# A recurrent layer with expert routing: another order of the first loads, softmax moved into the scan, more expert work inside the search

## The chip, the cores and the metric

The kernel runs on one core of one Trainium2 chip. The metric is the time of one execution on the device in microseconds (us); lower is better. The time before is the median of 3 runs.

## What is computed

A GRU runs over T = 256 steps with B = 16 sequences and D = 512 features. Its states go through a router with E = 16 experts in which each expert chooses its 256 best tokens of 4096; the experts share one weight matrix. All in float32. Cut to what matters:

```python
def cell(h, x):
    gi = x @ W_ih + b_ih                 # [16, 1536]
    gh = h @ W_hh + b_hh
    r = sigmoid(i_r + h_r); z = sigmoid(i_z + h_z)
    n = tanh(i_n + r * h_n)
    return (1 - z) * n + z * h
hs = scan(cell, cond, x over 256 steps)  # [16, 256, 512]

S = softmax(hs @ router_w + router_b)    # 4096 tokens x 16 experts
G, idx = top_k(S.T, 256)                 # each expert takes 256 tokens
y = scatter_add(idx, G * (hs[idx] @ expert_w + expert_b))
out = x + y
```

Since the expert matrix is shared, the kernel multiplies every token by `expert_w` once and scales the result by the sum of the weights that chose the token (its gate).

## The kernel before

**Tiles.** The 256 steps form NG = 32 groups of TG = 8 steps; a group is 128 rows (16 sequences x 8 steps). `xs` holds x and later the output by group, `ht` the transposed states by group, `lg` the router's logits and later the softmax, `wih` and `whh` the two weight matrices of the GRU, `ewr` the router's and the experts' weights. The input of the scan comes a second time, in another layout: `xa`, loaded by pairs of steps (4 pairs in a group), turned on VectorE into `xT` (`turn_x`, L255). `xa` has one buffer, so the load of the next group's `xa` waits for the turn of the last.

**Order.** The order within the engines is written out by hand (`manual_schedule`), for the head on SyncE, ScalarE and GpSimd (L264), then TensorE and VectorE (L459), in the scan and behind it on all of them.

**Head.** SyncE and ScalarE issue the weights (`load_rows`, L230). GpSimd issues pair 0 of x (`load_pair`, 4 loads, L268), three bias loads (L284), the condition's four (L287) and pair 1 of x (4 loads); SyncE issues pairs 2 and 3 behind the weights, then group 1 (`load_xa`, L238). GpSimd and SyncE can each have only a fixed number of loads under way before the next waits for one to land, as the profile shows. TensorE zeroes the PSUM banks of the gates with `begin_sums` (L112), is kept busy with more of it (`keep_clock`), multiplies pair 0 by the input weights (`x_part`, L429: 32 wide products `ra` for two gates, 32 narrow ones `zz`), makes the biases (`biases`, L310), and multiplies pair 1. VectorE turns pair 0, copies the biases (L472 to L474), turns pair 1 and then the condition (L479, L480), which is the first state.

**Scan.** In step s TensorE multiplies the state by the three gates' weights (`h_part`, L442), then does work for later: `x_part` of the next pair, logits of finished groups (L342) and a quarter of an expert product (`expert`, L391). ScalarE takes the sigmoid r (L504), two tanh (L555) and the sigmoid z (L556), and in even steps puts the biases into the next pair's banks (L406 to L417). VectorE does the products and turns (L508 to L576) that end in the next state. At the end of step c = 3 of a group it turns the next group's x (L595).

**Expert products.** 15 early groups are multiplied inside the scan. The other 17, the late groups, are multiplied behind it, in parts of 256 columns and one eighth of a group: `late_part` (L139, four products, one for each quarter of the PSUM rows). A late group needs a PSUM tile that `late_begin` zeroes (if fresh) and presets with the expert bias (L159, ScalarE); there are five tiles in turn, two of the pool `ps_m` and three of `ps_e`. `expert_for(n)` emits n parts at that point of TensorE's order. A finished group is copied by ScalarE to `ht` (L176), or, once the gate is known, read by VectorE from PSUM.

**Behind the scan.** The last logits (L356), 4 parts, exponential and sum of the 28 old groups (`exp_sum`, L621, L622), the last 4 groups' logits less their maximum (`less_max`, L368 to L374), the old groups' reciprocal and product (`softmax`, L614, L616), then the same for the 4 new groups. TensorE transposes the result (L728, L729).

The search finds each expert's 256th largest weight bit by bit, in 17 rounds (bits 27 to 11, `by_bits`): VectorE counts the weights not below a candidate (L655), TensorE adds the counts over an expert's rows (L670), VectorE drops or keeps the bit (L673, L678). In each round TensorE has 2 or 3 expert parts beneath:

```python
top = by_bits(KNOWN, HIGH, LOW, counts, lambda bit: expert_for(2 + bit % 2))
```

Then the exact threshold is made from the largest of the rest (L738 to L756), and the gate (L698, L702). From there `store` writes group after group: VectorE adds gate times product to x (L708) and SyncE issues the write (L711), early groups first, then the late ones as their parts end. Ahead of the last three groups the count is checked once more: VectorE counts, TensorE sums (L775), VectorE compares, TensorE sums again (L779); a flag chooses whether a slow exact path runs (it does not here).

Of the kernel before, what the change touches and what calls it, by code (L numbers as in the profile page):

```python
# [18 lines left out]
def kernel(  # L19
# [112 lines left out]

    def late_part(g, pe, part):

        k, h = divmod(part, 2)
        cols = slice(HD * h, HD * (h + 1))
        for j in range(KC):
            q = slice(QD * j, QD * (j + 1))
            nc.tensor.matmul(  # L139
                pe[q, cols],  # L140
                ht[:, g, k, q],
                ewr[:, k, E:][:, cols],
                start=False,
                stop=(k == KC - 1),
                tile_position=(0, QD * j),
                skip_group_check=True,
            )

    late = []
    late_sums = {}  # L150
    late_done = []
    gated = []

    def late_begin(pool, fresh=True):
        g = late_groups[len(late_done) + len(late)]
        pe = pool.tile([P, D], F32, name="pe", tag="pe")
        if fresh:
            begin_sums(pe)
        nc.scalar.copy(pe, eb)  # L159
        late.append((g, pe))  # L160

    def late_parts():
        for i, g in enumerate(late_groups):
            _, pe = late[0]
            for part in range(2 * KC):
                late_part(g, pe, part)
                if part == KC and i + 2 < len(late_groups):
                    n = (i + 2) % 5
                    late_begin(ps_m if n < 2 else late_pool[0], fresh=i < 3)
                if part == 2 * KC - 1:  # L170
                    late.pop(0)
                    late_done.append(g)
                    if gated:
                        late_sums[g] = pe
                    else:
                        nc.scalar.copy(wide(g), pe)  # L176
                yield

# [8 lines left out]
    with (  # L187
# [25 lines left out]

        ra = [ps_g.tile([P, 2, P], F32, name=f"ra{i}") for i in range(2)]
        hn = [ps_g.tile([P, 2 * P], F32, name=f"hn{i}") for i in range(2)]
        zz = [ps_g.tile([P, P], F32, name=f"zz{i}") for i in range(2)]

# [46 lines left out]
        with tc.manual_schedule(engines={ET.SP, ET.Activation, ET.Pool}):  # L264
            def load_pair(p, qs):

                for j in range(KC):
                    qs[j % 2].dma_start(  # L268
                        out=xa0[quadrant(j), p, :],
                        in_=x[:, 2 * p : 2 * p + 2, j * P : (j + 1) * P].rearrange("b o d -> o b d"),  # L270
                    )

            for i, gate in enumerate((0, 2, 1)):
                load_rows(wih[:, :, i, :], w_ih[:, gate * D : (gate + 1) * D], "(p c) n -> p c n")
            for gate in (0, 2, 1):
                load_rows(whh[:, :, gate, :], w_hh[:, gate * D : (gate + 1) * D], "(c p) n -> p c n")

            load_pair(0, (nc.gpsimd, nc.gpsimd))
            for dst, src in (
                (b_raw[0:1], b_ih.rearrange("(o g d) -> o g d", o=1, d=D)),  # L280
                (b_raw[1:2], b_hh.rearrange("(o g d) -> o g d", o=1, d=D)),
                (b_n, b_hh[2 * D :].rearrange("(o d) -> o d", o=1)),
            ):
                nc.gpsimd.dma_start(out=dst, in_=src)  # L284
            nc.gpsimd.memset(c0, 0.0)
            for j in range(KC):
                nc.gpsimd.dma_start(  # L287
                    out=c0[QD * j : QD * j + B, :].rearrange("b (c i) -> b c i", c=KC), in_=columns(cond, j)
                )
            load_pair(1, (nc.gpsimd, nc.gpsimd))  # L290
            for p in range(2, TG // 2):
                load_pair(p, (nc.sync, nc.sync))
            for j in range(KC):
                load_xa(1, xa1, j, (nc.sync, nc.sync))
            nc.sync.dma_start(out=ewr[:, :, E:], in_=expert_w.rearrange("(c p) n -> p c n", c=KC))
            nc.sync.dma_start(out=ewr[:, :, 0:E], in_=router_w.rearrange("(c p) n -> p c n", c=KC))
            nc.sync.dma_start(out=rb, in_=router_b.rearrange("(o e) -> o e", o=1).to_broadcast([P, E]))
            nc.sync.dma_start(out=eb, in_=expert_b.rearrange("(o d) -> o d", o=1).to_broadcast([P, D]))
# [67 lines left out]
        def less_max(h, pl):  # L366
# [12 lines left out]
            )  # L379

        pes = {}

# [76 lines left out]
        with tc.manual_schedule(engines={ET.PE, ET.DVE}):  # L459
            for i in range(2):  # L460
                for bank in (ra[i].rearrange("p g d -> p (g d)"), hn[i], zz[i]):
                    begin_sums(bank)
            keep_clock(22)
            turn_x(0, xa0, slice(0, 1))
            for z in (False, True):
                for k in range(KC):
                    x_part(0, k, z)
            keep_clock(2)
            biases(1)
            biases(0)  # L470
            keep_clock(2)
            nc.vector.tensor_copy(bias[:, 0:2, :], ra[1])  # L472
            nc.vector.tensor_copy(nb, hn[1][:, 0:P])
            nc.vector.tensor_copy(bias[:, 2, :], zz[1])  # L474
            turn_x(0, xa0, slice(1, 2))
            for z in (False, True):
                for k in range(KC):
                    x_part(1, k, z)
            nc.vector.transpose(turned, c0)  # L479
# [8 lines left out]
        with tc.manual_schedule(engines={ET.PE, ET.Activation, ET.DVE, ET.Pool, ET.SP}):  # L488
# [4 lines left out]
            for s in range(T):  # L493
# [38 lines left out]
                if s == T - 1:  # L532
                    logits(hn[0][:, P:], range(KC), range(NG - 1, NG), slice(0, TG - 1))


# [71 lines left out]
                if s in (T - 6, T - 4):  # L607
                    late_begin(ps_m)


            old, new = slice(0, NG - KC), slice(NG - KC, NG)

            def softmax(gs):
                nc.vector.reciprocal(tot[:, gs], tot[:, gs])  # L614
                n = gs.stop - gs.start
                nc.vector.tensor_tensor(  # L616
                    lg[:, :, gs], lg[:, :, gs], tot[:, gs].unsqueeze(1).to_broadcast([P, E, n]), ALU.mult
                )

            def exp_sum(gs):  # L620
                nc.scalar.activation(lg[:, :, gs], lg[:, :, gs], AF.Exp)  # L621
                nc.vector.tensor_reduce(tot[:, gs], lg[:, :, gs].rearrange("p e g -> p g e"), AX.X, ALU.add)  # L622

# [3 lines left out]
            )  # L627
            expert_for(4)
            exp_sum(old)
            less_max(NG // KC - 1, hn[0][:, P:])  # L630
            softmax(old)
            exp_sum(new)
            softmax(new)


    with (
# [69 lines left out]

        def store(g, sums, gate):
            nc.vector.scalar_tensor_tensor(  # L708
                xs[:, g, :], sums, gate[:, g : g + 1], xs[:, g, :], ALU.mult, ALU.add
            )  # L710
            nc.sync.dma_start(out=out[:, g * TG : (g + 1) * TG, :], in_=xs[:, g, :])  # L711

# [10 lines left out]
        with tc.manual_schedule(engines={ET.PE, ET.Activation, ET.DVE}):  # L723
# [8 lines left out]
            nc.vector.tensor_copy(by_block[:, KC - 1], ps_last.rearrange("p (q i) -> p q i", q=QG))  # L732

            counts = ps_c.tile([P, HIGH - LOW + 1], F32, name="counts")
            top = by_bits(KNOWN, HIGH, LOW, counts, lambda bit: expert_for(2 + bit % 2))

# [30 lines left out]
            gated.append(True)  # L767
            for i, g in enumerate([g for g in range(NG) if g not in late_groups] + late_groups):
                while g in late_groups and g not in late_done:
                    expert_for(1)  # L770
                store(g, late_sums.get(g, wide(g)), gate)
                if i == NG - 4:

                    n = ps_n.tile([P, 1], F32, name="n", tag="n")
                    nc.tensor.matmul(n, same_h, count(kth, "cnt"), start=True, stop=True)  # L775
                    wrong = wk.tile([P, 1], F16, name="wrong")
                    nc.vector.tensor_scalar(wrong, n, float(TOPK), None, ALU.not_equal)
                    n_wrong = ps_n.tile([1, 1], F32, name="n_wrong", tag="n")
                    nc.tensor.matmul(n_wrong, wrong, wrong, start=True, stop=True)  # L779
                    nc.vector.tensor_copy(flag, n_wrong)  # L780

        again = nc.values_load(flag, min_val=0, max_val=P)
        with tc.If(again > 0):
# [54 lines left out]
            for g in range(NG):  # L838
                sums = wide(g)
                if g in late_sums:  # L840
                    sums = ps_e.tile([P, D], F32, name="pe", tag="pe")
                    begin_sums(sums)
                    nc.scalar.copy(sums, eb)
                    for part in range(2 * KC):
                        late_part(g, sums, part)
                store(g, sums, gate)
# [31 lines left out]
```

## Time and profile before

| what | value |
|---|---|
| median of 3 runs | 1173.38 us (1172.32 to 1174.1) |
| the profiled execution | 1174.32 us, of which its span is 1172.5 us |
| mean granted TensorE clock | 0.994 |
| TensorE busy | 1150.8 us, 98% of the span |
| VectorE busy | 702.3 us, 60% |
| ScalarE busy | 332.7 us, 28% |
| first product with a state (L442) | 23.37 us from the span's start |
| last state written (L576) | 1090.62 us |
| transposes behind the softmax (L728) | 1094.80 us |
| last expert product ends | 1166.75 us |

The profile is one execution. Times are from the start of the span. A row of the timeline gives start, duration, engine, line, operation, what is written from what, how often, and in brackets how long the engine was idle before and what released it. Rows of one line that follow each other are merged, so the duration of a row with x24 spans all of them. A float32 product of TensorE is two records.

### The profile page before, as it was taken

The numbers are of one execution on the slowest core, as the hardware profiler recorded it, in microseconds if no ns is written. First come the engines' busy times: TensorE is split into PE (matmuls) and PEld (weight loads), VectorE is DVE, ScalarE is ACT, GpSimd is POOL, SyncE is SP. The second block draws the span as 40 slices with busy tenths as digits, with TensorE's granted clock in tenths as the row PEclk, the third lists the DMA queues.
The fourth block names the chain that finished last, engine by engine and source line by source line (L and its number), as shares of the span: only waits on it lengthen the run. The fifth ranks groups of instructions, "written<-read, shape, count | busy, mean of one in ns | idle before, by whom it ended". The sixth has DMA issues, their size and how long they took to land.

```text
span 1172.5 us, 79871 instructions
## 1 busy us (share of the span) xinstructions
PE 1150.8 (98%) x36285; PEld 1018.5 (87%) x36285; DVE 702.3 (60%) x4077; ACT 332.7 (28%) x1438; POOL 99.9 (9%) x412
## 2 busy tenths in 40 slices
PE   8999999999999999999999999999999999999897
PEld 5899999999999999999999999999999999998454
DVE  1665665666566656666666566666665566656682
ACT  0223323322233323232323232323232323233211
POOL 3000010000000000000000000000000000000000
PEclk8999999999999999999999999999999999999999
DMA  7200000000000000000000000000000000000045
GB/s 231 73 23 20 20 18 23 20 21 20 21 20 20 20 21 20 20 21 20 21 20 20 20 21 20 20 20 22 19 21 20 21 21 19 20 14 13 3 127 164
DMA packets 48712, 38.04 MB, mean 32 GB/s; under 512 B 7952, under 2 KB 40528, under 8 KB 48368
## 3 DMA queue, kind: packets, MB, share of 16 engines
q1 hardware_dynamic: 46128, 29.56, 8.7%
q8 instruction: 285, 4.67, 1.6%
q10 hardware_dynamic: 1632, 3.15, 0.8%
q14 instruction: 59, 0.48, 0.1%
q0 software_dynamic: 608, 0.19, 0.1%
HBM read 24.47 MB, written 8.39 MB: 28 GB/s over the span
## 4 chain that ended last, share of the span: by engine, by line
PE 93%; DVE 3%; DMA 2%; issue 1%; ACT 0%; SPq 0%; POOL 0%; DVEq 0%; ACTq 0%; POOLq 0%
PE ra L442 19%; PE hn L442 19%; PE ra L429 19%; PE zz L442 19%; PE zz L429 9%; PE pe L391 4%; PE pe L139 3%; DMA xa<-in_x_dram 1%; DVE xs L708 1%; PE hn L342 1%; DVE ge L655 1%; SPq L238 0%; POOL xa L268 0%; DMA out_dram<-xs 0%; PE counts L670 0%
## 5 line engine op out<-in xcount | busy, mean ns | idle before, releaser
L442 PE MATMUL ra<-whh,hs 128*16 128x128 f32 (+1 forms) x8192 | 318.5, 273 | 2.9 <-DVE zT L565 1.7
L442 PE MATMUL hn<-whh,hs 128*16 128x128 f32 (+1 forms) x8192 | 318.3, 273 | 0.2
L429 PE MATMUL ra<-wih,xt 128*32 128x256 f32 x4096 | 270.4, 381 | 3.6 <-DVE xt L255 3.1
L442 PE MATMUL zz<-whh,hs 128*16 128x128 f32 (+1 forms) x8192 | 271.0, 273 | 0.0
L504 ACT ACTIVATE r<-ra 128x128 f32<-128x128 f32 x256 | 71.1, 278 | 616.3 <-PE ra L442 616.3
L442 PEld LDWEIGHTS ra<-whh,hs 128*16 128x16 f32 (+1 forms) x8192 | 229.9, 103 | 6.8 <-DVE hs L576 3.3
L508 DVE COPY seen<-r 1x1 f32<-1x1 f32 x256 | 36.3, 142 | 330.3 <-ACT r L504 330.3
L442 PEld LDWEIGHTS hn<-whh,hs 128*16 128x16 f32 (+1 forms) x8192 | 230.8, 103 | 2.2 <-DVE l L368 2.2
L442 PEld LDWEIGHTS zz<-whh,hs 128*16 128x16 f32 (+1 forms) x8192 | 227.5, 103 | 0.1
L429 PEld LDWEIGHTS ra<-wih,xt 128*32 128x32 f32 x4096 | 128.5, 111 | 50.2 <-DVE xt L255 4.0
L555 ACT ACTIVATE t<-t 128x64 f32<-128x64 f32 x512 | 102.9, 248 | 131.7 <-DVE t L553 131.7
L429 PEld LDWEIGHTS zz<-wih,xt 128*32 128x32 f32 x4096 | 117.8, 110 | 23.3 <-DMA wih<-in_L_cond_W_ih_dram 1.3
L429 PE MATMUL zz<-wih,xt 128*32 128x128 f32 x4096 | 136.6, 274 | 0.4 <-DMA wih<-in_L_cond_W_ih_dram 0.4
L562 DVE STREAM_TRANSPOSE nT<-t 128x64 f32<-128x64 f32 x512 | 100.3, 234 | 49.5 <-ACT t L555 49.5
L565 DVE STREAM_TRANSPOSE zT<-zs 128x64 f32<-128x64 f32 x512 | 121.4, 237 | 0.2 <-issue 0.2
L576 DVE TENSOR_TENSOR hs<-v,nT 128x32 f32<-128x32 f32 x512 | 101.5, 198 | 21.7
L573 DVE TENSOR_TENSOR v<-u,zT 128x32 f32<-128x32 f32 x512 | 104.3, 204 | 8.9
L391 PE MATMUL pe<-ewr,ht 128*32 128x128 f32 x1920 | 93.8, 273 | 0.0
L551 DVE TENSOR_TENSOR t<-r,hn 128x64 f32<-128x64 f32 x512 | 89.5, 216 | 0.0
L553 DVE TENSOR_TENSOR t<-t,ra 128x64 f32<-128x64 f32 x512 | 87.9, 213 | 0.0
L568 DVE TENSOR_TENSOR u<-hs,nT 128x32 f32<-128x32 f32 x512 | 78.2, 153 | 0.0
L391 PEld LDWEIGHTS pe<-ewr,ht 128*32 128x32 f32 x1920 | 59.5, 110 | 19.4
(112 smaller groups left out, 569.4 us busy)
## 6 DMA issues: line engine op xcount, KB each, us to landing
xs<-in_x_dram SPq DMA_DIRECT2D x128, 64.0 KB
out_dram<-xs SPq DMA_DIRECT2D x32, 256.0 KB
xa<-in_x_dram SPq DMA_DIRECT2D x248, 32.0 KB
wih<-in_L_cond_W_ih_dram SPq DMA_DIRECT2D x3, 512.0 KB
wih<-in_L_cond_W_ih_dram ACTq DMA_DIRECT2D x3, 512.0 KB
whh<-in_L_cond_W_hh_dram SPq DMA_DIRECT2D x3, 512.0 KB
whh<-in_L_cond_W_hh_dram ACTq DMA_DIRECT2D x3, 512.0 KB
ewr<-in_L_ffn_expert_w_dram SPq DMA_DIRECT2D x1, 1024.0 KB
```

The costliest lines, as they stand in the source:

```text
L391: nc.tensor.matmul(pes[g][quadrant(j), at : at + P], ht[:, g, k, quadrant(j)], ewr[:, k, E + P * quarter : E + P * (quarter + 1)], start=( ...
L429: nc.tensor.matmul(dst, lhs, rhs, start=False, stop=(k == KC - 1), tile_position=(0, QD * j), skip_group_check=True)
L442: nc.tensor.matmul(dst[quadrant(j, m)], lhs, columns(whh[:, k, gate_, :], j), start=False, stop=(k == KC - 1), tile_position=(0, QD * j), ...
L504: nc.scalar.activation(r, ra[p % 2][:, 0, :], AF.Sigmoid)
L551: nc.vector.tensor_tensor(t[half], r[:, cols], hn[p % 2][:, cols], ALU.mult)
L553: nc.vector.tensor_tensor(t[half], t[half], ra[p % 2][:, 1, cols], ALU.add)
L555: nc.scalar.activation(t[half], t[half], AF.Tanh)
L562: nc.vector.transpose(nT[half], t[half])
L565: nc.vector.transpose(zT[half], zs[:, halves[half][1]])
L568: nc.vector.tensor_tensor(u[half], hs[:, halves[half][2], slot(s), :], of_step(nT[half], odd), ALU.subtract)
L573: nc.vector.tensor_tensor(v[half], u[half], of_step(zT[half], odd), ALU.mult)
L576: nc.vector.tensor_tensor(hs[:, halves[half][2], slot(s + 1), :], v[half], of_step(nT[half], odd), ALU.add)
```

## The change

Four things are altered.

1. In the head, GpSimd issues the three bias loads first, then pairs 0 and 1 of x interleaved (8 loads), then the condition. SyncE's 8 loads of pairs 2 and 3 are interleaved in the same way. TensorE makes the biases first, then the wide products of both pairs, then the narrow ones, then two rounds of clock keeping. The six gate banks are whole tiles of 512 columns and are zeroed whole.
2. The softmax of the 28 old groups runs in four stages at the end of steps 240 to 243 (exponential; sum; reciprocal; product), with a sigmoid of one element behind the exponential. Behind the scan only the 4 new groups are left.
3. Late parts: one in each of steps 254 and 255, 5 behind the scan, 2 behind the transposes, 3 in every round of the search. PSUM tiles after the first two are not zeroed again. `late_begin` for the group after next is called when a group ends, not in its middle. Once the gate is known a product has 512 columns.
4. The last late group is done in two halves of 256 columns, each with its own store. The check of the count is spread over the fifth, fourth and third groups from the end: its count, its first sum and its second sum stand each behind another group's parts.

```diff
@@ late parts
+    late_items = [(g, whole) for g in late_groups[:-1]] + [(late_groups[-1], half) for half in halves_d]
-    def late_begin(pool, fresh=True):
+    def late_begin(pool, fresh=False):
@@ late_parts()
-        for i, g in enumerate(late_groups):
-            _, pe = late[0]
-            for part in range(2 * KC):
-                late_part(g, pe, part)
-                if part == KC and i + 2 < len(late_groups):
-                    n = (i + 2) % 5
-                    late_begin(ps_m if n < 2 else late_pool[0], fresh=i < 3)
+        for i, (g, cols) in enumerate(late_items):
+            pe = late[0]
+            for k in range(KC):
+                for part in [cols] if gated or cols != whole else halves_d:
+                    late_part(g, pe, k, part)
+                    if k == KC - 1 and part.stop == cols.stop:
+                        if i + 2 < len(late_items):
+                            late_begin(ps_m if (i + 2) % 5 < 2 else late_pool[0])
...
@@ gate banks
-        ra = [ps_g.tile([P, 2, P], F32, name=f"ra{i}") for i in range(2)]
-        hn = [ps_g.tile([P, 2 * P], F32, name=f"hn{i}") for i in range(2)]
-        zz = [ps_g.tile([P, P], F32, name=f"zz{i}") for i in range(2)]
+        banks = [ps_g.tile([P, D], F32, name=f"gates{i}") for i in range(6)]
+        ra = [bank[:, 0 : 2 * P].rearrange("p (g d) -> p g d", d=P) for bank in banks[0:2]]
+        hn = [bank[:, 0 : 2 * P] for bank in banks[2:4]]
+        zz = [bank[:, 0:P] for bank in banks[4:6]]
@@ loads
-            load_pair(0, (nc.gpsimd, nc.gpsimd))
             for dst, src in (  # the three biases
...
                 nc.gpsimd.dma_start(out=dst, in_=src)
+            load_pairs(0, 2, nc.gpsimd)
             nc.gpsimd.memset(c0, 0.0)
...
-            load_pair(1, (nc.gpsimd, nc.gpsimd))
-            for p in range(2, TG // 2):
-                load_pair(p, (nc.sync, nc.sync))
+            load_pairs(2, TG // 2 - 2, nc.sync)
@@ head on TensorE and VectorE
             keep_clock(22)
-            turn_x(0, xa0, slice(0, 1))
-            for z in (False, True):
-                for k in range(KC):
-                    x_part(0, k, z)
-            keep_clock(2)
             biases(1)
             biases(0)
-            keep_clock(2)
...
-            turn_x(0, xa0, slice(1, 2))
+            for pair in range(2):
+                turn_x(0, xa0, slice(pair, pair + 1))
             for z in (False, True):
-                for k in range(KC):
-                    x_part(1, k, z)
+                for pair in range(2):
+                    for k in range(KC):
+                        x_part(pair, k, z)
+            keep_clock(2)
@@ scan
+                if s >= T - 2:
+                    expert_for(1)
...
+                if T - 16 <= s < T - 12:
+                    softmax(slice(0, NG - KC), s - (T - 16))
+                    if s == T - 16:
+                        nc.scalar.activation(seen[0:1, 0:1], seen[0:1, 0:1], AF.Sigmoid)
@@ behind the scan
-            expert_for(4)
-            exp_sum(old)
+            expert_for(5)
             less_max(NG // KC - 1, hn[0][:, P:])
-            softmax(old)
-            exp_sum(new)
-            softmax(new)
+            for stage in range(4):
+                softmax(slice(NG - KC, NG), stage)
@@ search
+            expert_for(2)
             counts = ps_c.tile([P, HIGH - LOW + 1], F32, name="counts")
-            top = by_bits(KNOWN, HIGH, LOW, counts, lambda bit: expert_for(2 + bit % 2))
+            top = by_bits(KNOWN, HIGH, LOW, counts, lambda bit: expert_for(3))
@@ stores
+            items = [(g, whole) for g in early_groups] + late_items
...
+                step = i - (len(items) - 6)
+                if step == 1:
+                    nc.tensor.matmul(n, same_h, cnt, start=True, stop=True)
+                elif step == 2:
+                    nc.tensor.matmul(n_wrong, wrong, wrong, start=True, stop=True)
+                store(g, late_sums.get((g, cols.start), wide(g)), gate, cols)
+                if step == 0:
+                    cnt = count(kth, "cnt")
+                elif step == 1:
+                    nc.vector.tensor_scalar(wrong, n, float(TOPK), None, ALU.not_equal)
+                elif step == 2:
+                    nc.vector.tensor_copy(flag, n_wrong)
```

## The prediction

> **What bounds the kernel now.** I read the page first (the chain that ended last and the row of clock), then the head, one loop step and the tail in the timeline. The chain says whose time it is:
>
> ```profile
> PE 93%; DVE 3%; DMA 2%; issue 1%; ACT 0%; SPq 0%; POOL 0%; DVEq 0%; ACTq 0%; POOLq 0%
> ```
>
> TensorE's own stream sets the time, so an edit gains what it takes out of that stream or out of the holes in it. The holes are in the head and the tail. The head (start, duration, engine, line, what, idle before it):
>
> ```profile
> 8.33 0.54 POOL L287 DMA_DIRECT2D xs<-in_cond_dram  x1 [1.85 <-DMA xa<-in_x_dram]
> 10.68 2.48 POOL L268 DMA_DIRECT2D xa<-in_x_dram  x4
> 18.79 0.40 DVE L255 STREAM_TRANSPOSE xt<-xa 128x128 f32<-128x128 f32 x1 [1.30 <-DMA xa<-in_x_dram]
> 19.25 3.42 PE L429 MATMUL ra<-wih,xt 128*32 128x256 f32 x32 [0.77 <-DVE xt L255]
> 23.37 0.61 PE L442 MATMUL ra<-whh,hs 128*16 128x128 f32 x16
> ```
>
> GpSimd has eight loads under way; the ninth (8.33) waits for the first to land. So pair 1 of x leaves only at 10.68 and is turned at 18.79, and its 32 products take 3.42 us where 1.71 is the full-clock price (24 such take 1.29 in the loop's chain). The state reaches TensorE at 23.37. The loop, at step 240, on ScalarE:
>
> ```profile
> 1027.43 0.28 ACT L556 ACTIVATE zs<-zz 128x128 f32<-128x128 f32 x1
> 1028.11 0.26 ACT L417 COPY zz<-bias 128x128 f32<-128x128 f32 x1
> 1030.27 0.28 ACT L504 ACTIVATE r<-ra 128x128 f32<-128x128 f32 x1 [1.89 <-PE ra L442]
> ```
>
> ScalarE is free from 1028.37 to 1030.27: 1.90 us. The tail:
>
> ```profile
> 1089.22 1.28 ACT L621 ACT_TABLE_LOAD   x1
> 1090.52 0.58 ACT L621 ACTIVATE lg<-lg 128x448 f32<-128x448 f32 x1
> 1091.13 0.96 DVE L622 TENSOR_REDUCE tot<-lg 128x28 f32<-128x448 f32 x1 [0.25 <-ACT lg L621]
> 1092.00 0.31 DVE L368 STREAM_TRANSPOSE l<-hn 128x128 f32<-128x128 f32 x1
> 1094.80 0.60 PE L728 MATMUL ps<-ident,lg 128*128 128x128 f32 x3 [2.12 <-DVE lg L616]
> ...
> 1110.31 0.16 PE L670 MATMUL counts<-cnt,same_h 128*128 128x1 f16 x1 [0.24 <-DVE ge L655]
> 1111.84 0.18 PE L670 MATMUL counts<-cnt,same_h 128*128 128x1 f16 x1
> 1113.25 0.16 PE L670 MATMUL counts<-cnt,same_h 128*128 128x1 f16 x1 [0.24 <-DVE ge L655]
> ...
> 1127.91 15.32 PE L139 MATMUL pe<-ewr,ht 128*32 128x256 f32 x280
> 1142.95 3.22 ACT L159 COPY pe<-eb 128x512 f32<-128x512 f32 x5 [16.59 <-DVE xs L708]
> 1155.77 0.16 PE L775 MATMUL n<-cnt,same_h 128*128 128x1 f16 x1 [1.60 <-DVE ge L655]
> 1156.19 10.56 PE L139 MATMUL pe<-ewr,ht 128*32 128x256 f32 x192
> ```
>
> Look at three things. TensorE idles 2.12 us before the transposes, behind the softmax of 28 old groups. A round of the search takes 1.53 us with three expert parts (1110.31 to 1111.84, TensorE-bound) and 1.41 with two (to 1113.25, where the count waits 0.24 us for VectorE). After the search TensorE is the bound to the end: 1127.91 to 1166.75, with the check of the count in its way (1154.16 to 1156.19).
>
> **Head: -0.65 us.** GpSimd now issues three bias loads, then the eight of pairs 0 and 1, then the condition's four. Eight may be under way, so five of x leave by about 6.1 us and the other three wait for the biases. Bias loads landed 6.6, 6.6 and 7.4 us after issue, so these three leave between 8 and 10, instead of up to 13.2 for the last of x now. That one landed in 5.5 us after its issue; I put x at 15 to 15.6. The condition's loads move behind it: issued by about 13, landed by about 19, with 0.5 us of turning: hidden if products last beyond 20. SyncE's eight loads keep their waits on weights. TensorE then does the biases at about 9, idles some 5 us, and from 15.3 has 64 wide (3.42 us at full clock) and 64 narrow products (1.74). An idle of 2.28 us (8.52 to 10.80) was followed, by the granted clock in windows of 1 us, by half clock from 12 to 15.3, so I let the first 3.6 us run at half clock, to 18.9: 1.8 us of work done, 3.36 left, two clock-keeping rounds 0.42: the state's product at 22.7 against 23.37. Ends: x a microsecond earlier gives -1.2; half clock until 20.4, or x at 16.5, gives 0 to +0.3. The wider zeroing of six banks (+0.7 us) lies before the biases land. A gain here passes on: pairs 2 and 3 leave SyncE by 24.2 and are turned at 32.1 without a wait, and the second group's load waits for that turn, so the later stall (turn at 40.43) moves along.
>
> **Loop: +1.5 us.** At step 240 ScalarE adds, behind its presets, a table load, the exponential, a table load back and a 1x1 sigmoid: 1.28 + 0.58 + 1.28 + about 0.2 (estimate, nearest row: the smallest ACTIVATE, 0.25) = 3.4 from 1028.37, so r of step 241 starts at 1031.77 instead of 1030.27. Behind it wait VectorE's gate chain and the next state. The first half of the state was there at 1032.58 and TensorE took it at 1032.85, so 0.27 is covered and TensorE stalls 1.23. Here a rule speaks against the change. The Trainium skill, ScalarE: Activation LUTs, What ACT_TABLE_LOAD costs, counts 2.66 us for a switch, the 1.28 of the load and a drain of 1.38. The trace has the 1.28 (1089.22), yet zs ends at 1089.21 and the exponential starts at 1090.52: no drain beside it. By the rule the two switches add 2.8 us more, a stall of 4.0; I take the trace's and keep the other as the end of the range. VectorE's share: the sum (0.96) at step 241 and the reciprocal (0.32) at 242 fit the gap between the state (r + 2.93) and the next gate (r + 4.44). At step 243 the turn of x ends at r + 4.30 and the product (0.62) behind it delays the next gate by 0.5, of which 0.27 is covered: +0.25. One part each in steps 254 and 255 fills holes of 0.42 and 0.49 with 0.44: +0.1, told with the tail.
>
> **Tail: -10.4 us + 0.1.** Softmax: the last table load stays hidden (it starts before the state is ready). l can start at 1091.0, when the last logits are done; to the end of lg 1.12 us as now, exponential 0.29, sum to product 0.75, 0.14 to TensorE: transposes at 1093.3 instead of 1094.8, -1.5. The five parts beneath end at 1093.1.
>
> Search: first count 2.02 us after the transposes as now, 1095.3; two new parts (0.88) fit under it. Sixteen periods of 1.535 = 24.56, instead of 25.25 (1096.82 to 1122.07): the eight rounds with a third part cost 0.12 each, +1.0; the zeroing of three banks goes (0.7 with its slow start); and the two first rounds (2.70 and 1.73 at half clock after 3.4 us of holes) become full-clock ones, since those holes are filled. From last count to the run at 1127.91 nothing changes, 5.84. So the run starts at 1125.7, 2.2 earlier.
>
> Rest: 53 of 136 parts are done there now, 83 follow in 36.46 us (15.32 + 10.57 + 10.57): 0.439 each. Changed: 2 + 5 + 2 + 51 + 6 = 66 done, 70 left = 30.75. Matmuls of 512 columns cost what two of 256 do (128 columns took 0.218, 256 took 0.44: no fixed part to save). The check no longer stops TensorE (its inputs come a group earlier): -2.0, its two products remain, 0.2. The wait for a PSUM bank stays: VectorE must write 23 groups (0.667 each) before the first that frees a bank, TensorE has 38 parts for that time: 0.4, as now. TensorE ends at 1125.7 + 30.75 + 0.6 = 1157.1, not 1166.75: -9.7. Behind it, half a group is stored instead of one: VectorE 0.75 to about 0.4, and the transfer 2.69 to about 2.35 (128 KB less at the 0.3 to 0.4 us that they take at 307 to 400 GB/s): -0.7.
>
> **Sum.** -0.65 + 1.5 + 0.1 - 10.4 = -9.45. Against the profiled execution: span 1172.5 and 1.82 around it, 1174.32, so 1164.9. That execution stands 0.94 above the median 1173.38; from the median the sum gives 1164.0, my time.
>
> **The rivals.**
> - As worked out, 0.76: 1164.0, own range 1161 to 1167.
> - The switch has the drain, or three parts in each round cost 1.7 instead of 1.535 (+2.6), 0.10: 1166.7. For it: a round's TensorE work is nearly all of its period. Against: three-part rounds of 1.53 stand in the trace.
> - The writes become the bound, 0.09: 8.39 MB leave from 1126.5 on. At the 307 GB/s that the windows of 10 us show from 1140 to 1150 that is 27.3 us, before TensorE's end; at 271 (1130 to 1140) 31 us and the last store queues behind it: about +2.5, 1166.5.
> - Slower, 0.03: the clock stays at half in the search. A three-part round then takes about 3.0, 1.5 more; from the seventh such round on the gain is gone, and with all 17 it is 1189. For it: rounds 27 and 26 ran so. Against: the same windows have the granted clock at 1.00 from 1110 on with a TensorE less loaded than it will be.
> - The reorder in the head and the steps' parts do less than said, and all the tail's small terms fail, 0.02: 1172, no change.
>
> **How the numbers follow.** 0.2% (2.3 us) is about what a measurement of this kernel can tell from no change. Faster: 0.76 + 0.10 + 0.09 = 0.95; same 0.02; slower 0.03. The range for 8 in 10: the head from -1.2 to +0.3, the loop from +0.8 to +4.3, the tail from -11.3 to -9.0, not all at one end: 1160.8 to 1167.8.
>
> **What would show it.** Right: pair 1 turned at 15 to 16; the state's first product near 22.7; two table loads at step 240 and one TensorE hole of about 1.2 us behind; transposes 2.7 us after the last state instead of 4.2; all counts 1.53 apart; 35 us from the start of the long run of parts to the end of the span (now 44.6), with no count check in front of parts. Wrong: rounds of 1.7 or more, a drain of more than a microsecond beside a table load, a last store that waits for earlier ones, or a clock of 0.5 after 1097.

## The result, and the profile after

| | before | changed |
|---|---|---|
| median | 1173.74 us (1172.32 to 1176.06, 4 runs) | 1164.78 us (1164.32 to 1165.21, 4 runs) |
| ratio | | 0.9922 [0.9904, 0.9939] |
| profiled execution | 1174.32 us, span 1172.5 | 1164.63 us, span 1162.8 |
| mean granted TensorE clock | 0.994 | 0.996 |

The change takes 8.96 us between the medians, where the working summed to 9.45. To see whether its steps were right, I cut both spans at the same instructions ("r" is ScalarE's first sigmoid of a step). In us:

| stretch | before | changed | difference | forecast |
|---|---|---|---|---|
| start of the span to the first sigmoid r | 24.93 | 25.26 | +0.33 | -0.65 |
| to r of step 6 | 25.26 | 24.05 | -1.21 | 0 |
| to r of step 240 | 975.99 | 976.26 | +0.27 | 0 |
| to the last state | 64.44 | 65.46 | +1.02 | +1.6 |
| to the transposes | 4.18 | 2.70 | -1.48 | -1.5 |
| to the first count | 2.02 | 2.01 | 0 | 0 |
| 16 search periods | 25.25 | 24.66 | -0.59 | -0.7 |
| to the start of the run of parts | 5.84 | 5.86 | 0 | 0 |
| run to the end of TensorE | 38.84 | 31.23 | -7.61 | -7.5 |
| end of TensorE to end of the span | 5.78 | 5.27 | -0.51 | -0.7 |
| sum | | | -9.8 | -9.45 |

The search and the run of parts make the gain, within 0.2 us of the working. The head's forecast is wrong in sign in this profile, and the second row has a gain that was not forecast. The +0.27 of the third row is chance: a second execution of the changed kernel takes 975.99 there.

The timeline of VectorE and TensorE in the head, changed kernel:

```profile
15.42 0.40 DVE L258 STREAM_TRANSPOSE xt<-xa 128x128 f32<-128x128 f32 x1 [4.00 <-DMA xs<-in_cond_dram]
15.88 7.56 PE L445 MATMUL gates<-wih,xt 128*32 128x256 f32 x128 [4.03 <-DVE xt L258]
16.39 0.41 DVE L258 STREAM_TRANSPOSE xt<-xa 128x128 f32<-128x128 f32 x1 [0.57 <-DMA xa<-in_x_dram]
```

(In the first row the label names the condition's load; it is a load of x that landed at 15.40.) Both pairs of x are turned by 16.8, where pair 1 was turned only by 19.2. But TensorE idles 4.03 us, and its products (128 records) then take 7.56 us. The windows of the same kernel (stretch, length, then busy time of TensorE, its weight loads, VectorE, ScalarE and GpSimd with counts, the granted clock, DMA share, GB/s) say why:

```profile
19.00:20.00 1.00, 1.00 (x16) 0.45 (x12) 0.43 (x3) 0.00 (x0) 0.00 (x0) 0.50 1.04 385
20.00:21.00 1.00, 1.00 (x20) 0.55 (x16) 0.00 (x0) 0.00 (x0) 0.00 (x0) 0.85 0.83 289
```

The clock is at half until about 20.3 (0.85 in the second window is half for 0.3 of it), and full from there on.

Step 240 on ScalarE, and TensorE's hole behind it:

```profile
1027.50 0.26 ACT L433 COPY gates<-bias 128x128 f32<-128x128 f32 x1
1027.78 1.28 ACT L388 ACT_TABLE_LOAD   x1
1029.07 0.58 ACT L388 ACTIVATE lg<-lg 128x448 f32<-128x448 f32 x1
1029.65 1.28 ACT L627 ACT_TABLE_LOAD   x1
1030.95 0.20 ACT L627 ACTIVATE seen<-seen 1x1 f32<-1x1 f32 x1
1031.06 0.25 ACT L516 ACTIVATE r<-gates 128x128 f32<-128x128 f32 x1
```
```profile
1033.33 2.81 PE L458 MATMUL gates<-whh,hs 128*16 128x128 f32 x96 [0.92 <-DVE hs L590]
```

The four added instructions lie end to end, and r of the next step starts right behind them.

TensorE behind the scan:

```profile
1093.73 0.60 PE L731 MATMUL ps<-ident,lg 128*128 128x128 f32 x3 [0.20 <-DVE lg L395]
...
1095.74 0.16 PE L673 MATMUL counts<-cnt,same_h 128*128 128x1 f16 x1 [0.30 <-DVE ge L658]
1095.84 1.50 PE L137 MATMUL pe<-ewr,ht 128*32 128x256 f32 x24
1097.27 0.18 PE L673 MATMUL counts<-cnt,same_h 128*128 128x1 f16 x1
...
1126.26 16.52 PE L137 MATMUL pe<-ewr,ht 128*32 128x256 f32 x160
1143.27 3.64 PE L137 MATMUL pe<-ewr,ht 128*32 128x512 f32 x32 [0.49 <-ACT pe L160]
1146.84 0.18 PE L780 MATMUL n<-cnt,same_h 128*128 128x1 f16 x1
...
1150.40 0.17 PE L783 MATMUL n_wrong<-wrong 128*1 128x1 f16 x1
```

The 2.12 us before the transposes are 0.20. The first counts start 1.53 us apart (1095.74 to 1097.27), and three parts (x24, 1.50 us) fill all of a round. The check's two products (1146.84 and 1150.40) stand between parts without a wait; the only hole left from 1126.26 on is the 0.49 us for a PSUM bank.

### The profile page after: what moved, and what is told of

It is laid out like the page before. It is cut to its first block, busy times and chain, and to the rows that moved or that the text cites. A ratio compares the mean times of both kernels' runs of the same rounds, so it can differ in the third digit from the quotient of the medians.

```text
span 1162.8 us, 79365 instructions
## 1 busy us (share of the span) xinstructions
PE 1147.7 (99%) x36025; PEld 1018.4 (88%) x36025; DVE 703.6 (61%) x4078; ACT 336.1 (29%) x1444; POOL 100.0 (9%) x412
## 5 line engine op out<-in xcount | busy, mean ns | idle before, releaser
L458 PE MATMUL gates<-whh,hs 128*16 128x128 f32 x24576 | 723.2, 273 | 3.4 <-DVE hs L590 3.3
L458 PEld LDWEIGHTS gates<-whh,hs 128*16 128x16 f32 x24576 | 675.6, 103 | 9.5 <-DVE hs L590 4.1
L445 PE MATMUL gates<-wih,xt 128*32 128x256 f32 (+1 forms) x8192 | 385.7, 327 | 4.0 <-DVE xt L258 4.0
L445 PEld LDWEIGHTS gates<-wih,xt 128*32 128x32 f32 x8192 | 256.0, 110 | 65.9 <-DVE xt L258 4.3
L516 ACT ACTIVATE r<-gates 128x128 f32<-128x128 f32 x256 | 71.1, 278 | 614.1 <-PE gates L458 614.1
L565 DVE TENSOR_TENSOR t<-r,gates 128x64 f32<-128x64 f32 x512 | 89.7, 217 | 0.0
L567 DVE TENSOR_TENSOR t<-t,gates 128x64 f32<-128x64 f32 x512 | 88.4, 214 | 0.0
L570 ACT ACTIVATE zs<-gates 128x128 f32<-128x128 f32 x256 | 71.0, 277 | 0.0
L137 PE MATMUL pe<-ewr,ht 128*32 128x256 f32 (+1 forms) x848 | 64.5, 442 | 0.5 <-ACT pe L160 0.5
L333 POOL COPY ht<-hs 128x128 f32<-128x128 f32 (+1 forms) x128 | 46.8, 396 | 160.9 <-DVE hs L590 153.1
L249 POOL COPY xs<-hs 1x1 f32<-1x1 f32 x128 | 22.7, 178 | 338.5 <-DVE hs L590 333.5
L137 PEld LDWEIGHTS pe<-ewr,ht 128*32 128x32 f32 x848 | 25.9, 109 | 27.0 <-issue 16.8
```

Of the source, the lines that this page charges most:

```text
L137: nc.tensor.matmul(pe[q, cols], ht[:, g, k, q], ewr[:, k, E:][:, cols], start=False, stop=(k == KC - 1), tile_position=(0, QD * j), skip_g ...
L445: nc.tensor.matmul(dst, lhs, rhs, start=False, stop=(k == KC - 1), tile_position=(0, QD * j), skip_group_check=True)
L458: nc.tensor.matmul(dst[quadrant(j, m)], lhs, columns(whh[:, k, gate_, :], j), start=False, stop=(k == KC - 1), tile_position=(0, QD * j), ...
L565: nc.vector.tensor_tensor(t[half], r[:, cols], hn[p % 2][:, cols], ALU.mult)
L567: nc.vector.tensor_tensor(t[half], t[half], ra[p % 2][:, 1, cols], ALU.add)
```

## The experiments

The runs were made in three groups, at three times. Differences are against the changed kernel, which ran again beside the second group: 1164.85 us (1164.21 to 1165.28, 5 runs), against 1174.37 before, 0.9916 [0.9903, 0.993]. Its medians differ by 0.07 us between the two occasions, and single runs by about 1.1 us, so I read medians to some 0.5 us and leave finer questions to the trace. The kernel before had medians of 1174.35, 1174.37 and 1173.54 beside the three groups. The third group (the last group whole, four parts, the bank's store first, all together) thus stands about 0.8 us low, and there the ratio to the kernel before (0.9916 for the changed kernel) says more than the median. The diffs are shortened to what matters.

> The changed kernel once more, as the measure for the others of this group. All theories: 1164.3 to 1165.5; the first gate r between 24.9 and 25.4 us, depending on when the full clock comes in the head; no stop of TensorE of a microsecond between 40 and 50 us if that stop depends on where the expert weights' load stands, a stop in some executions if it is chance.

### The head: is it the order, or the clock?

**Old order of loads and products.** Everything else of the change stays.

```diff
-            keep_clock(22); biases(1); biases(0)
-            (both pairs of x turned; wide products of both; narrow products of both; keep_clock(2))
+            keep_clock(22); turn_x(pair 0); products of pair 0; keep_clock(2)
+            biases(1); biases(0); keep_clock(2)
+            turn_x(pair 1); products of pair 1
```

> The changed kernel with the old head: pair 0 of x, biases, condition, pair 1 from GpSimd, products of pair 0 ahead of the biases. Theory A (the order of the loads does not matter, since TensorE runs the products at half clock behind its idle time in either head): first gate r at 24.9 instead of 25.26 us, end within 0.4 us of the changed kernel's 1164.8. Theory B (the reorder is worth the forecast's 0.65 us and the profiled execution hit a late clock): 0.5 to 0.8 us slower, 1165.4.

Measured 1164.55 us (1164.4 to 1164.99), 0.9916 [0.9903, 0.993]. The first r starts at 25.11 with the old order, and at 24.15 to 25.79 in nine executions with the new one (mean 24.93; before: 24.93). So the reorder gives nothing that can be told. By the profiles of the kernel before and of the changed one the products start 3.37 us sooner (15.88 instead of 19.25), but the products of both pairs stand behind that point instead of one pair's (+2.6), two rounds of clock keeping too (+0.4), and half clock lies on 4.4 us of them instead of 3.1 (+0.7).

**Fill the idle stretch.** Seventeen more rounds of zeroing stand behind the biases.

```diff
             biases(0)
+            keep_clock(17)
```

> The changed kernel with 17 more zeroings of the idle bank on TensorE between the biases and the first products, which fill most of its idle time from 11.9 to 15.9 us. Theory A (half clock is what ate the head's gain): granted clock 1.0 through the head, 128 products in about 5.2 us instead of 7.56, first gate r about 2.3 us earlier, and as much off the end: 1162.5. Rival (the recurrent weights land only near 22 us, or the later wait for the second group's x swallows it): 1164.0 to 1164.8.

Measured 1163.04 us (1162.41 to 1163.78), 0.9902 [0.9886, 0.9917]: 1.7 less than the changed kernel, and their ranges don't meet. TensorE of this kernel in the head, and one of its windows (columns as above):

```profile
11.88 3.87 PE L112 MATMUL idle<-zero 128*32 128x512 bf16 x68
15.71 5.70 PE L445 MATMUL gates<-wih,xt 128*32 128x256 f32 x125
```
```profile
18.00:19.00 1.00, 1.00 (x28) 0.57 (x24) 0.89 (x6) 0.00 (x0) 0.30 (x1) 1.00 1.05 385
```

The products start at the same time as without it (15.71 against 15.88), with the clock at 1.00 and the DMAs as busy, and r starts at 23.32, 1.94 earlier. That half clock costs the head these 1.9 us is shown by taking it away. The old order with a filled stretch was not run, so whether the new order is needed for this gain stays open.

**The gain that no step forecast.** Between r of step 5 and r of step 6 the kernel before took 5.15 us, since TensorE stopped; the changed kernel's profile has 4.20 there and no such row. But the second execution of the identical changed kernel has it too (5.05). The kernel before, then that execution:

```profile
47.29 0.41 PE L429 MATMUL ra<-wih,xt 128*32 128x256 f32 x2 [0.58 <-issue]
```
```profile
47.41 0.96 PE L445 MATMUL gates<-wih,xt 128*32 128x128 f32 x26 [0.69 <-issue]
```

"issue" says that the profile shows nothing TensorE waited for. From the first r to r of step 6 it took 24.91 us here and 24.05 in the first execution. So the -1.21 of the table's second row is, but for the -0.26 below, no effect of the change.

The nearest suspect was the 1 MB load of the expert weights, which is issued at 37.6 and with which the DMAs are full from 40 to 42. I split it into four quarters of the columns, three of them issued in steps 8 to 10, on top of the filled head:

```diff
+            keep_clock(17)
...
-            nc.sync.dma_start(out=ewr[:, :, E:], in_=expert_w...)
+            load_expert(0)
...
+                if s in (8, 9, 10):
+                    load_expert(s - 7)
```

> The changed kernel with 17 more zeroings in the head (as e2) and the expert weights' 1 MB load in four quarters: the first where the whole stood, the others in steps 8 to 10. Theory A (while that 1 MB and the second x group fill the DMA engines, TensorE's instructions arrive late, which cost e2 1.0 us in step 4): no stop between 38 and 50 us, the whole of the head's 1.9 us reaches the end: 1162.4 or less, 2.3 us under the changed kernel of this group. Rival (the stop is chance, or has another cause): a stop of about 1 us again, 1163.0 to 1163.8.

Measured 1162.59 us (1162.16 to 1162.93), 0.9898 [0.9882, 0.9913]: 0.45 below the filled head alone, of other runs on another chip. The first r to r of step 6 took 24.45 us; in the last kernel below, which spreads the load too, 24.80, with this line:

```profile
43.18 1.74 PE L464 MATMUL gates<-whh,hs 128*32 128x128 f32 x56 [0.51 <-issue]
```

The stop is still there without the large load. It comes and goes by up to 1.1 us between executions.

What TensorE waits for can be read from the DMA records of the same traces, which list the engines' instructions as well. One queue (q8, kind `instruction`) brings blocks of 16 KB, 283 in the changed kernel; with its 72 thousand records TensorE is the only engine with so long a stream, some 255 records to a block. Six of the profiles have a row of this kind (kernel before, second execution, filled head, spread load, bank's store first, all together). In five of them TensorE stops behind exactly 1985 of its records, in the sixth (bank's store first) behind 1729, which is 256 fewer, though these are different places in different programs. And it goes on 1.33 to 1.36 us (in the sixth 1.51) after the next block has landed, which starts 5.0 to 6.8 us behind the one before where 3.9 is the median of the scan. By these counts TensorE had run out of instructions, which is the wait that theory A names. Why the block is late is not shown: the full DMAs are the likely reason, but it is late with the split load too.

### The old groups' softmax: steps 240 to 243 or behind the scan

**Back behind the scan.** The block in the steps is dropped.

```diff
-                if T - 16 <= s < T - 12:
-                    softmax(slice(0, NG - KC), s - (T - 16))
...
+            softmax(old, 0); softmax(old, 1)
             less_max(NG // KC - 1, hn[0][:, P:])
+            softmax(old, 2); softmax(old, 3)
```

> The changed kernel with the softmax of the 28 old groups behind the scan again, in the old order, and no table switch at step 240. Theory A (moving it won 1.5 us in the tail and cost 1.1 in the loop): step 241 without its hole, 1.1 us earlier; transposes 4.2 us behind the last state instead of 2.7; 0.4 us slower, and up to 1.0 more if the hole ahead of the transposes brings half clock into the first rounds: 1165.2 to 1166.2. Rival (the move itself is no gain): 1164.3 or less.

Measured 1164.45 us (1163.75 to 1165.01), 0.9914 [0.99, 0.9928]. The steps from 240 on take 64.44 us again instead of 65.46, and the transposes come 4.18 behind the last state instead of 2.70. TensorE's wait before them in this kernel:

```profile
1093.57 0.60 PE L731 MATMUL ps<-ident,lg 128*128 128x128 f32 x3 [1.69 <-DVE lg L395]
```

So the move costs 1.02 in the scan and gives 1.48 behind it: 0.46 us net by the trace, which the medians cannot tell from nothing. The 16 periods took the same 24.66, so the idle 1.69 cost no clock.

**One step later.** In odd steps ScalarE has no presets to do.

```diff
-                if T - 16 <= s < T - 12:
+                if T - 15 <= s < T - 11:
```

> The changed kernel with the four softmax stages in steps 241 to 244 instead of 240 to 243: the table switch then stands in an odd step, where ScalarE has no presets to do behind its second sigmoid. Theory A (what costs is the ScalarE work beyond the time up to the next r): ScalarE is free at r + 1.6 instead of r + 2.2, the next r is 0.75 to 0.8 us late instead of 1.4, TensorE's hole 0.5 instead of 1.1: 0.6 us faster than the changed kernel of this group. Rival (the two loads cost 1.1 wherever they stand): no change.

Measured 1163.84 us (1162.74 to 1165.23), 0.9908 [0.9894, 0.9921]. ScalarE of this kernel:

```profile
1030.94 0.28 ACT L570 ACTIVATE zs<-gates 128x128 f32<-128x128 f32 x1
1031.24 1.28 ACT L388 ACT_TABLE_LOAD   x1
```

The load follows the sigmoid z at once, without the three presets between them, and the steps from 240 on take 64.90 us instead of 65.46. The 0.56 is read from the trace; the ranges of the times overlap.

### Parts in the search: two, three or four in a round

```diff
-lambda bit: expert_for(3)
+lambda bit: expert_for(2 + bit % 2)
```

> The changed kernel with two and three parts in turn in the rounds, as before, so 8 parts less in the search. Theory A (TensorE is the bound from the search to the end): eight rounds 0.13 us shorter each, -1.0, and 8 parts of 0.44 more behind the gate, +3.5: 2.5 us slower, 1167.3. Rival (the writes are the bound at the end, or three parts stretch a round by more than 0.13): no slower than 1165, or faster.

Measured 1166.3 us (1165.68 to 1166.76), 0.993 [0.9917, 0.9944]: 1.5 more than with three. The rounds take 23.52 instead of 24.66, the run of parts 34.00 instead of 31.23. TensorE's run in this kernel is one row up to the check, with no wait for a bank:

```profile
1125.03 23.41 PE L137 MATMUL pe<-ewr,ht 128*32 128x256 f32 x224
```

Eight parts more would be 3.5 us; the run grew by 2.77, since the wait of 0.49 went (0.2 stay unexplained). A part put into the search costs 1.14/8 = 0.14 us there and saves 0.35 to 0.44 behind it.

```diff
-lambda bit: expert_for(3)
+lambda bit: expert_for(4)
```

> The changed kernel with four parts in each round of the search instead of three, 17 parts more ahead of the gate. Theory A (TensorE is the bound from the search to the end and nothing else is near): rounds of 1.98 us, +7.0 in the search, -7.4 behind the gate, no change. Rival (the writes and VectorE's stores stand close behind TensorE): the gate comes 7 us later, 8.39 MB at about 310 GB/s need 27 us from there, and TensorE waits about 2 us for a bank: 1.5 to 2.5 us slower, 1166.3 to 1167.3.

Measured 1172.62 us (1171.22 to 1173.92), 0.9993 [0.9985, 1.0002]: 7.8 more than with three; by the ratio nothing of the change's gain is left. The rounds grew to 1.97 us, +6.9 in all, which 17 parts fewer should have repaid. They didn't: the run took 32.16 us for 53 parts. VectorE and TensorE of this kernel:

```profile
1132.52 16.65 DVE L711 SCALAR_TENSOR_TENSOR xs<-ht,gate,xs 128x512 f32<-128x512 f32 x25
```
```profile
1151.87 0.16 PE L780 MATMUL n<-cnt,same_h 128*128 128x1 f16 x1 [7.03 <-DVE ge L658]
1151.97 5.46 PE L137 MATMUL pe<-ewr,ht 128*32 128x512 f32 x32
```

VectorE has 25 groups to add to x (0.667 us each), and only behind them come the group that frees a PSUM bank and the check's count, for which TensorE waits 7.03 us. The wait also costs clock: the next 32 products take 5.46 us instead of 3.64. The sum closes: 31.23 less 7.5 for 17 parts and 0.49 for the wait that is gone, plus 7.03 and 1.82, is 32.1. The bound at this place is VectorE's order of stores.

### The check and the last group

**The check in one place again.** Its count, both sums and the comparisons stand together at the step that has the first sum.

```diff
-                if step == 0: cnt = count(kth, "cnt")      # and the second sum at step 2
-                if step == 1: matmul(n, same_h, cnt)
+                if step == 1: matmul(n, same_h, count(kth, "cnt")); wrong; matmul(n_wrong, wrong, wrong)
```

> The changed kernel with the check of the count in one place again, all of it behind the store of the fifth item from the end. Theory A (TensorE stood still for the check, and only for that): a hole of 1.6 to 2.0 us in the run of parts, the end later by as much: 1166.5 to 1166.8. Rival (the hole is covered by the bank wait or the writes): 1165.3 or less.

Measured 1167.13 us (1166.97 to 1167.53), 0.9937 [0.9923, 0.995]: 2.3 more than the changed kernel of the same group. TensorE of this kernel:

```profile
1149.13 0.16 PE L781 MATMUL n<-cnt,same_h 128*128 128x1 f16 x1 [1.61 <-DVE ge L658]
1149.55 0.16 PE L785 MATMUL n_wrong<-wrong 128*1 128x1 f16 x1 [0.25 <-DVE wrong L783]
```

The two holes are 1.86 us, and the run of parts is 1.97 longer (33.20): what the prediction took for this step, 2.0.

**The last group whole.**

```diff
-late_items = [(g, whole) for g in late_groups[:-1]] + [(late_groups[-1], half) for half in halves_d]
+late_items = [(g, whole) for g in late_groups]
```

> The changed kernel with the last late group in one piece of 512 columns and one store. Theory A (the halves only shorten what follows the last product): TensorE's end unchanged, 5.75 us from there to the end of the span instead of 5.3: 1165.3. Rival (the halves won nothing, or their second bank and second store cost as much): 1164.8 or less.

Measured 1167.37 us (1166.76 to 1168.9), 0.9949 [0.9936, 0.9963]. But this edit changed two things. With one item fewer, the check moves one group forward in TensorE's order, and its count is not made in time:

```profile
1143.81 0.16 PE L780 MATMUL n<-cnt,same_h 128*128 128x1 f16 x1 [2.50 <-DVE ge L658]
1143.91 5.34 PE L137 MATMUL pe<-ewr,ht 128*32 128x512 f32 x32
```

The 2.50 us of idle and the 32 products at half clock (5.34 instead of 3.64) are 4.2 us; less the wait of 0.49 for a bank, which is gone, that is 3.7, against the 3.5 by which the run of parts is longer (34.77). The loss is thus that of the check's place. For the halves themselves only the last stretch can be read: 5.43 us from the end of TensorE to the end of the span, against 5.27 and 5.40 in two executions of the changed kernel, and 5.15 to 5.76 over all kernels with halves. What they give cannot be told from nothing here, and is not the 0.7 of the forecast.

**The bank's store first.** Of the late groups' stores, the first that frees a PSUM bank is put ahead of those whose product is in `ht` already.

```diff
             items = [(g, whole) for g in early_groups] + late_items
+            items.insert(len(early_groups), items.pop(len(early_groups) + n_in_ht))
```

> The changed kernel in which VectorE stores the first late group that stays in PSUM ahead of the eight late groups that lie in ht, so its bank is free 5.3 us earlier. Theory A (TensorE's 0.49 us wait in the run of parts is for that bank alone): no wait there, end 0.5 us earlier, 1164.35. Rival (the next bank or the bias copy takes its place): no change.

Measured 1163.25 us (1162.53 to 1164.21), 0.9909 [0.9894, 0.9924]. TensorE of this kernel has one row, without a hole, from the start of the run to the check (1146.53):

```profile
1126.64 19.95 PE L137 MATMUL pe<-ewr,ht 128*32 128x256 f32 x192
```

The run takes 30.53 us instead of 31.23: the gain is these 0.7 us by the trace. The intervals of the two ratios overlap.

**All that helped, together**: the filled head with the spread load, the softmax one step later, and the bank's store first.

> The changed kernel with the warm head and the spread expert weights (as e11), the softmax at steps 241 to 244 (as e7) and the early store of the first PSUM group (as e12). Theory A (each removes a hole of TensorE at another place): the gains add, 2.3 + 0.6 + 0.5 = 3.4 us under the changed kernel, 1161.4. Rival (a chance stop of TensorE in the first 50 us, or the writes behind the last product, take part of it): 1162.0 to 1163.0.

Measured 1161.56 us (1160.17 to 1161.85), 0.9893 [0.9878, 0.9908]. It is the fastest kernel of the study, 12 us below the one before. Against the changed kernel it is 3.3 by the medians and 2.7 by the ratios, so the three gains add to most of the 3.4 forecast. Its first r starts at 22.88, and its run of parts takes 30.53.

## Why the prediction was right, and where not

- **Tail, right.** Transposes 2.70 us behind the last state (2.7 forecast), counts 1.54 apart on average (1.535), the run of parts 31.23 (30.75 + 0.6), and 36.5 from its start to the end of the span. For that the prediction's list of signs has 35, which is a slip: its own terms (30.75, 0.6, and 5.75 less 0.7) make 36.4. The two shares that could be tested alone came out at their price: the check 1.97 (2.0), and the wait for a bank 0.49 (0.4). Its only mis-sized term is the half group's store: 0.51 between the two profiles against 0.7, and the experiment could not attribute even that to the halves.
- **Loop, mechanism right, size 0.6 too high.** r came 1.40 us late (1.50 forecast), and TensorE took the state 1.09 later in its step, 0.92 of it as the hole in the row, against 1.23 forecast for the stall. The rule of the Trainium skill weighed there (ScalarE: Activation LUTs, What ACT_TABLE_LOAD costs) does not hold for these loads: the trace has 1.28 and then 0.01 to the next instruction, twice, and no drain. The +0.25 for step 243 did not come, and the parts in 254 and 255 (+0.1) cost nothing: from r to r, steps 240 to 244 took 20.71 us before and 21.75 now, step 243 among them 4.48 and 4.20, and the ten steps behind them are as long as before.
- **Head, the step that failed.** Two terms of the sum were too small. I took x to be ready for TensorE at 15.3. The last load of pair 0 landed at 15.40, about as forecast, but its turn on VectorE comes in between, and the products began at 15.88, 0.58 later. And I let the first 3.6 us run at half clock, to 18.9; half clock lasted to 20.3, 0.8 us longer on the products, which costs half of that, 0.4. Together that is the 1.0 between 22.7 and the 23.70 at which the state reached TensorE. The bound "half clock until 20.4" of the working, 0 to +0.3, was the right value: +0.33 in this profile, 0 in the mean of nine (against the one profile of the kernel before). The products ahead of the state ran at half clock in the old head too (the 3.42 us of the prediction's row, behind an idle of only 0.77); in the new one the idle ahead of them is 4.03. Filling that stretch gives 1.9 us in the trace and 1.7 by the medians, shown by experiment.
- **The shift of the later stall, right but small.** The second group's turn, which TensorE waits for near 40 us, costs 0.26 less (step 4 takes 3.90 us instead of 4.16).
- **A term by chance.** Of the profiled difference of -9.8, 0.95 is the stop near 47 us that the profile of before had and that of after had not. Without it and without the +0.27 of the third row the parts of the change sum to -9.1, and the medians say -8.96. In the sum of the profiles the head's error and this stop nearly cancel, so its good agreement with -9.45 is in part luck.
- **The rivals.** The clock stayed at 1.00 from the scan to the last product, so the slower case never began. The writes moved 311 and 331 GB/s in the two windows of 10 us from 1130 on, yet from 1126.26 to its end TensorE waited for nothing but the bank; they were not the bound. The table switch had no drain, and a round with three parts took no more than it did before.

The windows of the changed kernel for the writes (columns as above):

```profile
1130.00:1140.00 10.00, 10.00 (x96) 2.99 (x92) 10.00 (x16) 0.00 (x0) 0.00 (x0) 1.00 0.97 311
1140.00:1150.00 10.00, 9.51 (x93) 2.65 (x89) 6.71 (x12) 2.52 (x5) 0.00 (x0) 1.00 0.99 331
```

The DMAs are full for 20 us while TensorE is busy in 19.5 of them.

## What to carry to other kernels

Where one engine is busy to the end, count what is moved out of its last stretch into holes, and price it by the rate of that stretch: that part of the sum held to 0.2 us here. Stop moving when the engine behind it fills: the third part per round paid, the fourth turned a gain of 9 us into nothing, since VectorE's stores and the check behind them became the wait. Data that came earlier to an engine that had lost its clock brought nothing here; keep the clock first, then shorten the wait.

## What the runs showed of the hardware

- **An idle of 2.5 us cost the clock, holes of 1.6 and 1.7 us did not.** In the kernel with the last group whole, TensorE idled 2.50 us and its next 32 products took 1.70 longer; with four parts, 7.03 us of idle cost 1.82. That is half of a stretch of 3.4 to 3.6 us at half clock, however long the idle was. In the clock records of all these traces the stretches at half clock are 3.41, 6.83 or 10.24 us long (apart from the last one, which the kernel's end cuts off). The Trainium skill (TensorE: Matmul & The Clock Gate, What's actually happening) tells of an activity window of about 3.4 us, and these lengths, one, two and three of them, agree. The rule of the same page (HAM oscillation — how this bites in real kernels), no gaps above about 3.4 us, would have let the 2.50 pass; here the measurement decides. Holes of 1.61 and 1.69 us cost nothing: the first 24 products behind the one took 2.78 us, as in the changed kernel without that hole, and the 16 periods behind the other were as long as without it.
- **The length of a hole does not decide alone.** In the 3.41 us ahead of a possible change of the clock TensorE was busy for 1.08 us with the hole of 2.50 and half clock followed; it was busy for 2.00 and 1.73 us with the holes of 1.61 and 1.69 and the clock stayed. But in the head of the kernel before it was busy for 2.99 us (15.48 to 18.90), most of it with the biases' products of one and two rows, and half clock followed all the same. Whether such products count for less was not tested.
- **A table load on ScalarE took its 1.28 us and nothing else**: at step 240 it started 0.02 us behind the copy, and the exponential 0.01 us behind it.
- **TensorE can run out of instructions.** In six profiles it idles 0.3 to 1.1 us, 42 to 48 us after the start, always behind the same count of its records (once 256 fewer), until 1.3 to 1.5 us after the next 16 KB of instructions have landed. The profile calls this wait "issue". It is there in one execution of a kernel and not in another, so a difference of 1 us between two single profiles need not come from the edit.
